# A frequency-domain layer and a selective-scan layer on one core: the second layer's constants and first front issued in turns with the first layer's last synthesis, and a new order for the steady part

## The chip, the core and the metric

The kernel runs on one core of a Trainium2 chip. A core has five engines, each with its own queue of instructions in a fixed order: TensorE (PE: matrix products and transposes into PSUM), VectorE (DVE), ScalarE (ACT), GpSimd (POOL) and SyncE (SP, which here issues most DMAs). Engines wait for each other through semaphores. The metric is the device time of one execution in microseconds (us); lower is better.

## The reference

The input x is 4 images of 192 channels of 128 x 128 points, fp32. Two layers are computed, each as a residual:

```python
x = x + _L0_conv_ref(_gn(x), ...)   # layer 1 in the text: spectra
x = x + _L1_conv_ref(_gn(x), ...)   # layer 2 in the text: selective scan
```

`_gn` is a group norm over groups of 6 channels and all points of an image. The first layer makes 48 channels of the 192, sends 16 through a fractional Fourier transform and back, 16 through a real FFT and back, 16 past both, and projects to 192. The second layer takes each image as a sequence of 16384 tokens. Each token is layer-normed, projected to 384 channels u and 384 gates z; u passes a causal convolution of four taps and a silu. From u come a step size dt (softplus) for each channel and vectors B and C of 16 states for each token. The recurrence, for each of 384 x 16 states along the sequence, is

```python
dA = jnp.exp(dt_t[..., None] * A)
hnew = hcar * dA + (dt_t * u_t)[..., None] * B_t[:, None, :]
y_t = jnp.sum(hnew * C_t[:, None, :], axis=-1)
```

and then y + u * D, times silu(z), projected back to 192 channels, plus the residual.

## The kernel before, in words

**The first layer** (`layer0`) makes four passes per image: `analysis` (statistics and the projection to 48 channels), `forward` and `backward` (the transforms), and `synthesis`, which goes through an image in 16 pieces of 1024 points. For each piece synthesis loads x (`xt`, 768 KB) and the 48 channels (`cat`, four DMAs on SP, two buffers), makes four matrix products (L487), adds them to `xt` on VectorE (L491), takes bn_stats of the sum for the next norm (L202) and stores it to the DRAM tensor `xmid` (L495). `weave` mixes the passes of different images; the last one, synthesis of image 3, runs alone. After it come `bn_done` and `_group_stats`: a chain of small operations on VectorE, PE and ScalarE that gives the norm's mean and scale, `st2`.

**The second layer** (`layer1`) starts then: constants are loaded and prepared, and 128 chunks of 512 tokens follow, 32 to an image. A chunk has 384 channels in three tiles j of 128, 16 states for each: 48 scans of a 128 x 512 tile. They are done in 24 groups of two states; group k is tile j = k // 8 and states 2(k % 8) and 2(k % 8) + 1. The text calls k the place in the chunk. For one state the kernel does:

- the decay exp(dt A) on ScalarE (L875), into SBUF (`da`, AHEAD = 4 states ahead) or into PSUM (`op`);
- the input dt u B, in one of three ways that `KINDS` gives for each group: "V", VectorE multiplies a PSUM copy of dt u with the broadcast B (L896, "product"); "O", GpSimd multiplies both states at once into `db` (L907), with the decay in PSUM; "P", ScalarE scales a transposed dt u (L924, "scale", token by token) and PE transposes it back (L939, `turned_back`);
- the scan on VectorE (L953), into `h`, which has three buffers. The last column of each h is stored by a small DMA on SP as the next chunk's start (`carry`, L964);
- the product with C for both states on GpSimd (`hc`, L966), then the sum over states as transposes that accumulate in PSUM on PE (`sums`, L979, three groups late).

V and P inputs and O decays use three PSUM buffers named `op` in turn. B and C reach the core as a DRAM tensor `dbc`, stored from `xd` on ScalarE's output (`xd_out`) and read back, broadcast over 128 partitions, as up to two loads of 512 KB a group on SP (`load_bc`), at places 19 to 23 and 0 to 2. A new h must wait until both the GpSimd product and the carry store of the h three groups before are done.

**The front** of a chunk (loading `xm`, the norm as a matrix product `to_tokens`, `moments`, `rstd`, `shift`, `normed`, `to_channels`, `channels`, `conv`, `silu_u`, `proj_z`, `silu_z`, `proj_x`, `xd_out`, `proj_dt`, `softplus`, `dt_u`) and its **end** (`evacuate`, `turn`, `gate`, `project_out`, `add_x`) are spread by hand over the groups of the chunks before and after. `PLAN` says where: an entry (at, phase, name, arguments) is issued when the group is `at` places from the chunk's first, so that -35 is place 13 two chunks before. A group has four phases:

```python
act(pos, "S")
turned_back(G * (pos + 1))
... sums ...
act(pos, "A")
... inputs(*order[pos + 2]) ...
scans(pos, n, k, lambda: act(pos, "M"))   # M lies after the first of the two scans
act(pos, "L")
... load_bc ...
```

The order on each engine is this program order (`manual_schedule`), so what an entry puts on an engine stands ahead of all that is issued later. Five PSUM banks serve the plan's other tiles; `psum` takes the bank that was freed first. ScalarE switches its function table between log/exp, silu and softplus (L668, L778, L785, L815).

Of the kernel before, what the change touches and what calls it, by code (L numbers as in the profile page):

```python
# [52 lines left out]
def _group_stats(nc, small, psum, g_ones, mv, out, eps):  # L53

    ps = psum.tile([CH, 512], F32, name="ps")
# [6 lines left out]
    ps2 = psum.tile([CH, 512], F32, name="ps")  # L62
# [59 lines left out]
def layer0(tc, x, xmid, st2, w):  # L122
# [5 lines left out]
    with ExitStack() as ctx:  # L128
        def pool(name, bufs, **kw):
            return ctx.enter_context(tc.tile_pool(name=name, bufs=bufs, **kw))  # L130

        cp = pool("l0c", 1)
        dram = pool("l0d", B, space=DRAM)
        xp = pool("l0x", 7)
        sp = pool("l0s", 2)
# [6 lines left out]
        psB = pool("l0r", 2, space=PSUM)  # L142

        def const(name):
            src = w[name]
            t = cp.tile(list(src.shape), F32, name="c_" + name)
            nc.sync.dma_start(out=t, in_=src)
            return t

        g_ones, w1T, bd, bdb, rm = (const(k) for k in ("g_ones", "w1T", "bd", "bdb", "rowmask"))  # L150
# [5 lines left out]
        w2x = cp.tile([128, C], F32, name="w2x")  # L156
# [24 lines left out]
        cats = [cp.tile([128, 512], F32, name=f"cat{i}") for i in range(2)]  # L181
# [24 lines left out]
        def bn_done(st, out):  # L206
            mv = sp.tile([CH, 2, 2], F32, name="mv")
            for t in range(2):
                nc.vector.bn_aggr(mv[:, t, :], st[:, t, :, :])
            _group_stats(nc, sp, psA, g_ones, mv, out, 1e-5)  # L210
# [46 lines left out]
        def analysis(b, got):  # L257
# [11 lines left out]
            bn_done(st, gst)  # L269
# [3 lines left out]
            w1r = sp.tile([CH, 2, 128], F32, name="w1r")  # L273
# [7 lines left out]
            b1 = sp.tile([128, 1], F32, name="b1")  # L281
            nc.vector.tensor_scalar(b1, ps[:, 0:1], -1.0, None, ALU.mult)
            d1 = got["d1"] = dram.tile([3 * NC, S * S], F32, name="d1")
            for p in (*range(NPIECE - KEEP, NPIECE), *range(NPIECE - KEEP)):
                xt = kept.pop(p, None) or load(b, p)
                if p % 2 == 0:
                    x1 = sp.tile([128, 2, 512], F32, name="x1")
# [184 lines left out]
        def synthesis(b, got, early):  # L472

            d1, dimg = got["d1"], got["dimg"].rearrange("c h w -> c (h w)")
            st = sp.tile([CH, 2, NPIECE * (PIECE // 512), 6], F32, name="st2")
            for p in range(NPIECE):
                xt = early[p] if p < len(early) else load(b, p)
                cat = cats[p % 2]
                for q in range(2):
                    at = slice(p * PIECE + q * 512, p * PIECE + (q + 1) * 512)  # L480
                    nc.sync.dma_start(out=cat[64 * q : 64 * q + NC, :], in_=d1[0:NC, at])
                    nc.sync.dma_start(out=cat[64 * q + NC : 64 * q + 3 * NC, :], in_=dimg[:, at])
# [16 lines left out]
            bn_done(st, st2[:, b])  # L499
# [30 lines left out]
        weave([(synthesis(B - 1, got[B - 1], early), 1)])  # L530
# [4 lines left out]
KINDS = ("VOPPVVOP", "VOVPOVPP", "VOVPPVOP")  # L535

PLAN = (
    (-35, "M", "load_x"), (-34, "M", "to_tokens", 1), (-34, "L", "to_tokens", 0),
    (-33, "L", "moments", 0), (-32, "A", "moments", 1), (-31, "L", "rstd"), (-30, "M", "shift"),
    (-30, "M", "normed", 0), (-30, "M", "normed", 1), (-30, "M", "to_channels", 1),  # L540
    (-29, "L", "to_channels", 0), (-29, "L", "channels", 0), (-27, "L", "channels", 1),
    (-26, "S", "conv", 0, 0), (-26, "L", "conv", 1, 0), (-25, "L", "conv", 1, 1),
    (-24, "L", "conv", 1, 2), (-22, "S", "conv", 0, 1), (-20, "S", "silu_u", 1),
    (-20, "S", "conv", 0, 2), (-20, "S", "silu_u", 0), (-20, "M", "conv", 2, 0),
    (-19, "M", "conv", 2, 1), (-17, "A", "conv", 2, 2), (-16, "L", "silu_u", 2),
    (-15, "L", "proj_z", 0), (-15, "L", "silu_z", 0), (-13, "S", "proj_x"), (-13, "M", "xd_out"),
    (-11, "M", "proj_dt"), (-10, "S", "softplus"), (-9, "M", "dt_u", 1), (-8, "S", "turn_b"),
    (-8, "M", "dt_u", 0), (-8, "M", "b_out"), (-4, "A", "turned", 0), (-2, "M", "scale", 0, 6),
    (-2, "L", "dtu_copy", 0), (-1, "A", "scale", 0, 4), (0, "A", "scale", 0, 5),
    (0, "M", "scale", 0, 15), (1, "S", "scale", 0, 7), (2, "M", "scale", 0, 14),  # L550
    (4, "S", "turned", 1), (7, "A", "dt_u", 2), (7, "A", "dtu_copy", 1), (7, "A", "scale", 1, 6),
    (7, "M", "scale", 1, 7), (9, "M", "scale", 1, 15), (10, "S", "proj_z", 1),
    (10, "A", "scale", 1, 14), (10, "L", "scale", 1, 13), (10, "L", "scale", 1, 12),
    (10, "L", "evacuate", 0), (11, "S", "proj_z", 2), (11, "M", "silu_z", 1),
    (11, "M", "silu_z", 2), (11, "L", "turn", 0), (13, "S", "gate", 0), (13, "A", "dtu_copy", 2),
    (17, "S", "turned", 2), (17, "S", "scale", 2, 6), (17, "M", "scale", 2, 7),
    (18, "M", "scale", 2, 8), (18, "M", "scale", 2, 9), (18, "M", "evacuate", 1),
    (19, "L", "scale", 2, 15), (20, "S", "scale", 2, 14), (21, "A", "turn", 1),
    (22, "S", "gate", 1), (27, "A", "evacuate", 2), (29, "S", "turn", 2), (29, "M", "gate", 2),
    (32, "S", "project_out", 0), (32, "L", "add_x", 0), (34, "S", "project_out", 1),  # L560
# [4 lines left out]
def layer1(tc, xmid, out, st2, w, n_tok=S * S):  # L565
# [6 lines left out]
    AHEAD = 4  # L572
    NBLK = T // 128

    with ExitStack() as ctx:
        def pool(name, bufs, **kw):
            return ctx.enter_context(tc.tile_pool(name=name, bufs=bufs, **kw))

        cp = pool("l1c", 1)
        dram = pool("l1d", 3, space=DRAM)  # L580
# [4 lines left out]
        scp = pool("l1s", 4)  # L585
        op = pool("l1o", 1)
        ps1 = pool("l1p", 1, space=PSUM)
        psa = pool("l1a", 3, space=PSUM)
# [7 lines left out]
        banks = list(range(5))  # L596

        def psum(g, *key):
            bank = banks.pop(0)
            g[key] = ps1.tile([128, 512], F32, name=f"ps{bank}"), bank  # L600

        def done(g, *key):
            banks.append(g.pop(key)[1])
# [8 lines left out]
        nc.vector.scalar_tensor_tensor(  # L612
            nmr, st2[:, :, :, 0], -1.0, st2[:, :, :, 1], ALU.mult, ALU.mult
        )
        dnmr = dram.tile([CH, B, 2], F32, name="dnmr", bufs=1)
        nc.sync.dma_start(out=dnmr, in_=nmr)
        gd = cp.tile([CH + 1, B, 2, CH], F32, name="gd")
        for b in range(B):
# [4 lines left out]
        for b in range(B):  # L623
# [3 lines left out]
        xms = [cp.tile([CH + 1, 2, T], F32, name=f"xm{i}") for i in range(3)]  # L627
        for xm in xms:
            nc.vector.memset(xm[CH : CH + 1], 1.0)
# [40 lines left out]

        def load_x(i):
            b, ch = divmod(i, NCHUNK)
            xm = got[i]["xm"] = xms[i % 3]
            nc.sync.dma_start(
                out=xm[0:CH],
                in_=xmid[b][:, ch * T : (ch + 1) * T].rearrange("(t p) f -> p t f", p=CH),
            )
# [3 lines left out]
        def to_tokens(i, half):  # L681
            g = got[i]
            psum(g, "X", half)
            for blk in (2 * half, 2 * half + 1):
                for t in range(2):
                    nc.tensor.matmul(
                        row(g, blk)[:, t * CH : (t + 1) * CH],
                        g["xm"][:, t, blk * 128 : (blk + 1) * 128], gd[:, i // NCHUNK, t, :],
# [6 lines left out]
        def mean_var(g):  # L695
            return g["X", 1][0][:, 2 * C : 2 * C + 2 * NBLK].rearrange("p (k m) -> p k m", m=2)

        def moments(i, half):
            g = got[i]
            st = tp.tile([128, 2, 6], F32, name="st")  # L700
            for blk in range(2):
                nc.vector.bn_stats(st[:, blk, :], row(g, 2 * half + blk))
            for blk in range(2):
                nc.vector.bn_aggr(mean_var(g)[:, 2 * half + blk, :], st[:, blk, :])

        def rstd(i):
            g = got[i]
# [527 lines left out]
```

## Time and profile before

| | us |
|---|---|
| median of 3 runs (11174.6 to 11181.5) | 11175.6 |
| the profiled execution | 11188.6 |
| its span, first to last instruction | 11186.7 |
| first scan of the second layer | 1445.6 |
| one chunk, mean of 110 | 75.98 |

The page of a profile gives the busy time of each engine, the span in 40 slices, the chain of work that ended last, the costliest groups of instructions and the DMA issues. A line such as `h<-da,carry,op` names what is written and what is read. "Idle before" tells how long an engine stood still before an instruction, with the name of what ended the wait; when an instruction waits for several semaphores, the name is that of the one that came last by the profile, which need not be the one that it needed. PE is TensorE, PEld its weight loads, SPq and POOLq are DMA issues of SyncE and GpSimd.

### The profile page before, as it was taken

Reading aid. Unit: us, or ns where it says so; the run is one execution under the profiler, and the core shown is the slowest. Engines: PE = TensorE matmul, PEld = TensorE weight load, DVE = VectorE, ACT = ScalarE, POOL = GpSimd, SP = SyncE. Lnnn points to the kernel's source line nnn. Section 1 sums busy time; section 2 is a strip of 40 time slices with the busy share of each in tenths; the row PEclk is TensorE's granted clock in tenths of the full one; section 3 lists DMA queues with packets and bytes.
Section 4 is the critical chain, followed back from the end, with each engine's and each line's share of the span. In section 5 each row is a group of like instructions: output and inputs, shape, how many; then the busy total and the mean of one; then the engine's idle time right before and its main releaser. Section 6 shows DMA issues by size and latency. Waiting matters only on the chain. (4 is left out here: it accounts for less than half of the span.)

```text
span 11186.7 us, 171424 instructions
## 1 busy us (share of the span) xinstructions
PE 9950.4 (89%) x56050; PEld 6911.8 (62%) x56050; DVE 10160.0 (91%) x11330; ACT 9542.3 (85%) x20197; POOL 9513.5 (85%) x4342
## 2 busy tenths in 40 slices
PE   4777789999999999999999999999999999999998
PEld 2434356666666666666666666666666666666666
DVE  5666679999999999999999999999999999999999
ACT  2333189999999999999999999999999999999998
POOL 0000079999999999999999999999999999999999
PEclk8888699999999999999999999999999999999999
DMA  8786733333333333333333333333343333333333
GB/s 234 187 225 163 220 98 114 117 105 109 117 105 110 117 105 109 117 112 102 118 117 97 119 119 95 118 119 99 114 119 101 113 117 106 109 117 107 107 117 92
DMA packets 1330364, 1366.48 MB, mean 122 GB/s; under 512 B 918346, under 2 KB 969791, under 8 KB 1328831
## 3 DMA queue, kind: packets, MB, share of 16 engines
q1 hardware_dynamic: 1308990, 1292.60, 39.8%
q0 software_dynamic: 13312, 50.34, 1.4%
q10 hardware_dynamic: 7168, 12.59, 0.3%
q8 instruction: 445, 7.29, 0.3%
q14 instruction: 449, 3.67, 0.1%
HBM read 1179.79 MB, written 155.33 MB: 119 GB/s over the span
## 5 line engine op out<-in xcount | busy, mean ns | idle before, releaser
L966 POOL TENSOR_TENSOR hc<-h,c 128x1024 f32<-128x1024 f32 x3072 | 7200.0, 2367 | 321.2 <-DVE h L953 240.8
L953 DVE TENSOR_TENSOR_SCAN h<-da,carry,op 128x512 f32<-128x512 f32 x4464 | 5532.7, 1268 | 281.0 <-ACT op L875 122.6
L875 ACT ACTIVATE da<-dt,c_A_log 128x512 f32<-128x512 f32 x4608 | 3218.5, 741 | 224.7 <-DVE h L953 216.0
L979 PE MATMUL ps<-ident,hc 128*128 128x128 f32 x24576 | 3258.2, 278 | 3.7 <-POOL hc L966 3.7
L979 PEld LDWEIGHTS ps<-ident,hc 128*128 128x128 f32 x24576 | 2874.5, 144 | 277.2 <-issue 272.2
L924 ACT ACTIVATE dbT<-ps,bT 128x128 f32<-128x128 f32 x9216 | 2583.6, 396 | 12.6 <-PE op L939 11.7
L766 PE MATMUL ps<-s,wc 128*128 128x512 f32 x4608 | 2184.4, 596 | 44.0 <-ACT u L778 36.4
L953 DVE TENSOR_TENSOR_SCAN h<-op,carry,db 128x512 f32<-128x512 f32 x1488 | 1853.4, 1267 | 98.0 <-DMA carry<-h 81.7
L907 POOL TENSOR_TENSOR db<-dtu,b 128x1024 f32<-128x1024 f32 x768 | 1822.5, 2373 | 7.4 <-DMA b<-dbc 7.4
L939 PE MATMUL op<-ident,dbT 128*128 128x128 f32 x9216 | 1422.6, 281 | 242.8 <-ACT dbT L924 168.8
L939 PEld LDWEIGHTS op<-ident,dbT 128*128 128x128 f32 x9216 | 1107.4, 144 | 752.1 <-issue 334.6
L896 DVE TENSOR_TENSOR op<-ps,b 128x512 f32<-128x512 f32 x2304 | 1556.5, 676 | 7.2 <-ACT ps L856 7.2
L875 ACT ACTIVATE op<-dt,c_A_log 128x512 f32<-128x512 f32 x1536 | 1092.0, 711 | 267.4 <-DVE h L953 267.2
L766 PEld LDWEIGHTS ps<-s,wc 128*128 128x128 f32 x4608 | 786.1, 190 | 634.2 <-issue 565.9
L1018 PE MATMUL ps<-yg,c_woT 128*96 128x512 f32 x1536 | 710.2, 599 | 7.6 <-ACT u L778 2.1
L668 ACT ACT_TABLE_LOAD x511 | 655.6, 1283 | 10.0 <-PEq L1225 0.7
L916 PE MATMUL ps<-ident,dtu 128*128 128x128 f32 x1536 | 262.4, 297 | 337.0 <-ACT bT L834 337.0
L822 POOL TENSOR_TENSOR dtu<-dt,u 128x512 f32<-128x512 f32 x384 | 490.6, 1278 | 57.9 <-ACT dt L815 57.9
L495 POOL DMA_DIRECT2D xmid<-xt x64 | 41.6, 651 | 573.2 <-DVE xt L491 528.8
L1018 PEld LDWEIGHTS ps<-yg,c_woT 128*96 128x96 f32 x1536 | 240.2, 163 | 447.7 <-issue 336.7
L916 PEld LDWEIGHTS ps<-ident,dtu 128*128 128x128 f32 x1536 | 179.2, 148 | 393.2 <-ACT bT L834 366.8
L202 DVE BATCH_NORM_STATS2 st<-xt 96x6 f32<-96x512 f32 x512 | 322.2, 677 | 101.7 <-DMA xt<-in_x 100.5
(166 smaller groups left out, 9818.2 us busy)
## 6 DMA issues: line engine op xcount, KB each, us to landing
c<-dbc SPq DMA_DIRECT2D x1024, 512.0 KB, 5.8
b<-dbc SPq DMA_DIRECT2D x768, 512.0 KB, 4.9
xt<-in_x SPq DMA_DIRECT2D x176, 768.0 KB, 8.4
xmid<-xt POOLq DMA_DIRECT2D x64, 768.0 KB, 5.5
xm<-xmid SPq DMA_DIRECT2D x128, 384.0 KB, 3.8
carry<-h SPq DMA_DIRECT2D x3072, 1.0 KB, 1.9
out<-xm SPq DMA_DIRECT2D x128, 384.0 KB, 3.2
s<-s SPq DMA_DIRECT2D x128, 128.5 KB, 2.3
```

What stands on the lines that cost most here:

```text
L668: nc.scalar.preload_act_table_set("natural_log_exp_and_others")
L766: nc.tensor.matmul(g["c", j][0], wc[:, j, k, :], rhs, start=k == 0, stop=k == 5)
L822: nc.gpsimd.tensor_tensor(g["dtu", j], g["dt", j], g["u", j], ALU.mult)
L875: nc.scalar.activation(da, got[n]["dt", j], AF.Exp, scale=A[:, j, st : st + 1])
L896: nc.vector.tensor_tensor(dbs[s], g["dp", j][0], g["b", k % NG][:, q, :], ALU.mult)
L907: nc.gpsimd.tensor_tensor(db, _bc(g["dtu", j], 1, G), g["b", sg], ALU.mult)
L924: nc.scalar.activation(t[:, blk, :], g["tu", j][0][:, at], AF.Identity, scale=g["bT"][:, blk, st : st + 1],)
L939: nc.tensor.transpose(db[:, blk * 128 : (blk + 1) * 128], t[:, blk, :], ident)
L953: nc.vector.tensor_tensor_scan(h[:, q, :], das.pop(s), dbs.pop(s) if db is None else db[:, q, :], 0.0 if ch == 0 else g["before"][:, j, st ...
L966: nc.gpsimd.tensor_tensor(hc, h, g["c", "b", sg], ALU.mult)
L979: nc.tensor.matmul(py[:, blk, :], hc[:, q, blk * 128 : (blk + 1) * 128], ident, start=first, stop=sg == NG - 1 and q == G - 1 and blk == N ...
L1018: nc.tensor.matmul(g["po", t][0][0:CH], woT[:, j, t * CH : (t + 1) * CH], g["yg", j], start=j == 0, stop=j == NJ - 1,)
```

## The change

- `layer0` and `layer1` become generators. The pools of the first layer are split: those that the last synthesis needs stay open, the others are closed before it. The second layer's pools lie on the other side of the memory; its scan pools, one of its PSUM banks and the three `op` buffers are opened only after the last synthesis.
- `program` starts both, so that the second layer's constants are issued before the last synthesis, and then gives the second layer two places of its front after each of the 16 pieces. The front runs so far as place -3 (`LAST`); the group norm of image 3 follows. In the last synthesis the loads of a piece are issued one piece ahead. `_group_stats` takes its PSUM tiles from a function, which gives the last ones from another pool.
- In the steady part: `KINDS` changes for groups 12 (O to V), 20 (P to V) and 21 (V to P). `PLAN` is new throughout. `dbc_out` is an entry of its own, two places after `xd_out`. The residual is loaded a second time, late, into `xr` (28, "M"), and `xm` has one buffer instead of three. Decays in SBUF run seven ahead instead of four. `softplus` is split by tile. `moments` writes to SBUF instead of PSUM, and `rstd` computes its result twice, into SBUF and into PSUM.

In the instruction order of the changed kernel, SP issues 14 loads of B and C of chunk 0 ahead of the four `cat` loads of the last piece.

```diff
-KINDS = ("VOPPVVOP", "VOVPOVPP", "VOVPPVOP")
+BUFS = 7, 3
+
+KINDS = ("VOPPVVOP", "VOVPVVPP", "VOVPVPOP")
 PLAN = (
...
-    (-15, "L", "proj_z", 0), (-15, "L", "silu_z", 0), (-13, "S", "proj_x"), (-13, "M", "xd_out"),
-    (-11, "M", "proj_dt"), (-10, "S", "softplus"), (-9, "M", "dt_u", 1), (-8, "S", "turn_b"),
...
-    (7, "M", "scale", 1, 7), (9, "M", "scale", 1, 15), (10, "S", "proj_z", 1),
-    (10, "A", "scale", 1, 14), (10, "L", "scale", 1, 13), (10, "L", "scale", 1, 12),
-    (10, "L", "evacuate", 0), (11, "S", "proj_z", 2), (11, "M", "silu_z", 1),
...
+    (-15, "A", "proj_z", 0), (-15, "M", "silu_z", 0), (-13, "M", "proj_x"), (-12, "S", "xd_out"),
+    (-11, "M", "proj_dt"), (-10, "S", "dbc_out"), (-10, "A", "softplus", 0),
...
+    (9, "M", "scale", 1, 14), (10, "M", "scale", 1, 13), (10, "L", "scale", 1, 15),
+    (10, "L", "evacuate", 0), (10, "L", "proj_z", 1), (11, "M", "proj_z", 2),
...
+    (26, "M", "evacuate", 2), (28, "M", "load_xr"), (28, "L", "turn", 2), (30, "L", "gate", 2),
+    (31, "S", "project_out", 0), (32, "L", "add_x", 0), (34, "S", "project_out", 1),
...
-    AHEAD = 4
+    AHEAD, H = BUFS
...
-                decay(own[i], scp.tile([128, T], F32, name="da"))
+                decay(own[i], scp.tile([128, T], F32, name="da", bufs=AHEAD))
...
+        def load_xr(i):
+            xr = got[i]["xr"] = op.tile([CH, 2, T], F32, name="xr")
+            nc.sync.dma_start(out=xr, in_=chunk_of(xmid, i))
...
+        def dbc_out(i):
+            g = got[i]
             dbc = g["dbc"] = dram.tile([2, NS, T], F32, name="dbc")
-            nc.sync.dma_start(out=dbc.rearrange("a s t -> (a s) t"), in_=xd[96:, :])
+            nc.sync.dma_start(out=dbc.rearrange("a s t -> (a s) t"), in_=g["xd"][96:, :])
...
-            nc.scalar.activation(rs, mean_var(g)[:, :, 1], AF.Ln, bias=eps)
-            nc.scalar.activation(rs, rs, AF.Exp, scale=-0.5)
+            nc.scalar.activation(lnv, g["mv"][:, :, 1], AF.Ln, bias=eps)
+            g["rp"] = g["X", 1][0][:, 2 * C : 2 * C + NBLK]
+            nc.scalar.activation(rs, lnv, AF.Exp, scale=-0.5)
+            nc.scalar.activation(g["rp"], lnv, AF.Exp, scale=-0.5)
...
         def synthesis(b, got, early):
...
+            def fetch(p):
+                if p < NPIECE:
+                    cat = cats[p % 2]
+                    for q in range(2):
+                        at = slice(p * PIECE + q * 512, p * PIECE + (q + 1) * 512)
+                        nc.sync.dma_start(out=cat[64 * q : 64 * q + NC, :], in_=d1[0:NC, at])
+                        nc.sync.dma_start(out=cat[64 * q + NC : 64 * q + 3 * NC, :], in_=dimg[:, at])
+                if len(early) <= p + len(early) < NPIECE:
+                    xts.append(load(b, p + len(early)))
+
+            if early:
+                fetch(0)
             for p in range(NPIECE):
...
+                fetch(p + 1 if early else p)
...
-        weave([(synthesis(B - 1, got[B - 1], early), 1)])
+        inner.close()
+        yield
+        yield from synthesis(B - 1, got[B - 1], early)
...
             for pos in range(first, 0):
                 for phase in "SAML":
                     act(pos, phase)
                 if pos == -8:
                     for sg in range(NG):
                         load_bc(0, sg)
+                if pos <= LAST:
+                    yield pos == LAST
+                if pos == LAST:
+                    scp = pool("l1s", 4)
+                    op = pool("l1o", 1)
+                    ps2 = pool("l1q", 1, space=PSUM)
+                    psa = pool("l1a", 3, space=PSUM)
+                    banks.append(4)
+                    group_norm(B - 1)
...
-        layer0(tc, x, xmid, st2, w)
-        layer1(tc, xmid, [out[b].rearrange("c h w -> c (h w)") for b in range(B)], st2, w)
+        first = layer0(tc, x, xmid, st2, w)
+        second = layer1(tc, xmid, [out[b].rearrange("c h w -> c (h w)") for b in range(B)], st2, w)
+        next(first)
+        next(second)
+        ready = False
+        for _ in first:
+            for _ in range(2):
+                ready = ready or next(second)
+        for _ in second:
+            pass
```

## The prediction

> **What bounds the kernel now.** I read the page first, then busy time by stretch, VectorE's waits, and the timeline of one chunk and of the passage between the layers.
>
> ```profile
> span 11186.7 us, 171424 instructions
> PE 9950.4 (89%) x56050; PEld 6911.8 (62%) x56050; DVE 10160.0 (91%) x11330; ACT 9542.3 (85%) x20197; POOL 9513.5 (85%) x4342
> ...
> c<-dbc SPq DMA_DIRECT2D x1024, 512.0 KB, 5.8
> b<-dbc SPq DMA_DIRECT2D x768, 512.0 KB, 4.9
> ```
> The shares mix two layers. By stretch (columns: PE, weight loads, VectorE, ScalarE, GpSimd, clock, DMA share, GB/s):
> ```profile
> 1290.00:1310.00 20.00, 14.66 (x33) 4.62 (x29) 18.41 (x25) 0.00 (x0) 2.52 (x4) 0.50 0.95 279
> 1350.00:1370.00 20.00, 13.82 (x24) 4.35 (x20) 18.35 (x27) 0.00 (x0) 2.13 (x4) 0.50 0.69 211
> 1390.00:1410.00 20.00, 12.13 (x34) 7.53 (x35) 2.27 (x10) 8.00 (x13) 0.00 (x0) 0.55 0.03 7
> 1410.00:1430.00 20.00, 17.01 (x43) 6.95 (x42) 0.00 (x0) 6.37 (x9) 0.84 (x1) 0.96 0.10 25
> 1430.00:1450.00 20.00, 13.40 (x44) 8.55 (x44) 7.30 (x15) 12.80 (x33) 5.99 (x4) 0.70 1.00 354
> 5000.00:8000.00 3000.00, 2776.28 (x16289) 1977.01 (x16289) 2871.35 (x3164) 2834.53 (x6096) 2907.32 (x1306) 0.98 0.37 112
> ```
> The last synthesis (to 1370) keeps VectorE at 92% and the DMAs at 95%. Then VectorE and GpSimd stand nearly idle until the first scan at 1445.6. In the steady part (6144 scans, 48 to a chunk; 110 chunks give 75.98 us each) GpSimd is at 97%, VectorE 96%, ScalarE 94%, PE 93%: four engines in lockstep, so single waits matter. VectorE's, over 2000 to 11000 us:
> ```profile
> DVE h L953 <- ACT op L875: 119.3, 120, 1.4
> DVE h L953 <- DMA carry<-h: 101.4, 138, 1.9
> DVE h L953 <- PE op L939: 75.6, 139, 1.1
> DVE h L953 <- POOL hc L966: 33.1, 85, 1.4
> ```
> Summing the timeline's idle before each scan by its place in the chunk (group 0 to 23, mean of 110 chunks) gives 3.16 us a chunk: place 1 0.80, place 3 0.11, place 11 1.00, place 14 0.35, place 15 0.36, place 20 0.45, the rest 0.09. The name at place 11 misleads. One instance:
> ```profile
> 6044.06 2.81 PE L1018 MATMUL ps<-yg,c_woT 128*96 128x512 f32 x6
> ...
> 6046.72 1.02 PE L772 MATMUL ps<-s,wz 128*128 128x512 f32 x2
> 6047.58 1.02 PE L773 MATMUL ps<-s,wz 128*128 128x512 f32 x2
> ...
> 6048.44 0.60 PE L939 MATMUL op<-ident,dbT 128*128 128x128 f32 x4
> 6048.50 0.67 ACT L875 ACTIVATE op<-dt,c_A_log 128x512 f32<-128x512 f32 x1
> ...
> 6049.24 1.28 DVE L953 TENSOR_TENSOR_SCAN h<-da,carry,op 128x512 f32<-128x512 f32 x1 [0.99 <-ACT op L875]
> ```
> That ScalarE write belongs to group 12. Group 11 is a "P" group: its scan needs PE's transposes of 6048.44, which stood behind project_out and proj_z of place 10, phase S. They end at 6049.04; a scan starts some 0.2 us after its PE releaser.
>
> **What the Trainium skill says.** "DMA: Bandwidth & Descriptors", section "Queues, rings and completion order": each DMA engine takes a ring's descriptors in order. The trace agrees: a carry store lands 1.9 us after its issue at places 7 to 10, but 5.16 us at place 22, behind 512 KB B and C loads. "ScalarE: Activation LUTs", section "What ACT_TABLE_LOAD costs": 1283 ns a load (the trace: 1283) plus a drain of 1380 that no row here shows; the next activation starts some 10 ns later. "TensorE: Matmul & The Clock Gate", section "What's actually happening": PE runs at half clock until it is kept busy. The rows agree: 0.50 in the synthesis, 0.98 in the steady part.
>
> **Part 1, the kinds.** Group 12 goes from O to V; groups 20 and 21 swap P and V. GpSimd loses one db product a chunk (2.37 us, start to start 2.33): 0.968 x 75.98 - 2.33 = 71.2 us. VectorE gains two products: in the timeline one moves the next scan's start by 0.58 us, so +1.17. VectorE's work is 75.98 - 3.16 = 72.82, now 73.99: VectorE becomes the bound. ScalarE makes two decays in SBUF (741 ns) instead of PSUM (711) and one more 128x4 exponential (0.2 us); the instruction order holds the same eight table loads a chunk; it stays near 72 us. PE's count is the same, 70.3 us.
>
> **Part 2, the waits.** Place 11: proj_z moves behind the transposes (places 10 L and 11 M), 1.73 us less in front against a stall of 1.00: gone. Place 14 has two parts: 0.17 is the carry of place 11, whose issue waits 4.54 us on the SP queue behind the dbc store, which waits for xd (2.13 to land; 6.67 against the 6.5 us of places 12 and 13). dbc_out now comes two places after xd_out and has nothing to wait for. 0.14 is a late decay; seven ahead instead of four adds three states, over 3.5 us, more than a table switch. Left 0.03. Place 20: group 20 needs no transposes any more and GpSimd is lighter; left 0.10. Place 15 (two P groups in a row, PE late) stays: 0.36. Place 1 is the carry of place 22: issue 1.49 after its scans, behind the s store and two B and C loads, 5.16 to land, 6.65 against 5.9 us of places 23 and 0. That order on SP stays; ScalarE reaches the s store a little earlier: 0.60. GpSimd's sum for places 20 to 1 (two db products in six places) makes it about 0.4 late there, in the same wait, not on top. Places 3 and the rest: 0.21. Sum 1.30, chunk 73.99 + 1.30 = **75.29**, gain 0.69 x 128 = **88 us**. Bounds: no idle left gives 73.99 (-255); all 3.16 left gives 77.15 (+150).
>
> **Part 3, small edits, at nothing.** The second read of the residual is 128 loads of 384 KB where the DMAs are 37% busy, issued at place 4 and used at place 8; uncovered it would cost its landing, 3.8 us a chunk. One xm buffer instead of three: loaded at 13 M, read at 14 L, at least 3.5 us of scans and more on PE; what is uncovered would delay the transposes queued behind. bn_aggr writing SBUF (187 ns to PSUM before) may be 0.05 us either way, four times a chunk, beside idle; up to 26 us over the kernel each way.
>
> **Part 4, the front.** Before: the last bn_stats ends at 1367.0, the statistics at 1371.3, the first scan is at 1445.6 and the first chunk takes 83.5 us where later ones without start-up waits and carries would take 73.0 (48 scans 0.06 shorter): 78.6 + 10.5 = 89 us after the synthesis. After, on the path:
> - the constants (17 SP issues, 2.4 MB at 280 GB/s, 8.6 us) stand before the last image's first pieces, half of them in DMA time that is idle now: +4;
> - VectorE, the bound of the pieces, gets 4.4 us of moments and 2.9 us of weight products: +7;
> - 14 B and C loads (7.3 MB at the 354 GB/s of 1430:1450, 21 us) are issued on SP ahead of the last piece's four loads, while two pieces of 5.2 us are left to compute: +11. This is the queue that the move is dear on;
> - the last image's norm sends two small DMAs on SP ahead of the first carry stores; both are ready with the statistics, and the new pools' first tiles wait for the last stores of the first layer (5.5 us from issue to landing, the last issued near 1365, so before 1371): 0;
> - statistics 4.3, then two table loads (2.6), copies, a scaling, a decay and a product (3.7), start-up waits 3: +14.
>
> Together 36 against 89: 53 gained. PE may be late while both streams share it at a low clock, so I take **45**, with 15 and 70 as ends.
>
> **Sum.** 88 + 45 = 133. The profiled execution took 11188.6 (span 11186.7); the median, 11175.6, is 13 lower and I take the difference off the median: **11043 us**.
>
> **Rivals.**
> *The likeliest*, 0.57: chunk 74.9 to 75.7 with a front gain of 25 to 65: 10973 to 11115.
> *VectorE almost never waits*, 0.13: the seven decays and the lighter GpSimd close nearly all gaps, chunk 74.4: 1.58 x 128 + 45 = 247, 10929. For it: GpSimd drops from 97 to 95%. Against it: four engines above 93% with three-deep h and PSUM buffers.
> *The front alone*, 0.18: waits move to other places, 3.16 - 1.17 = 1.99 us stay, chunk 75.98, only 45 gained: 11131, up to 11155.
> *The front buys nothing*, 0.04: the synthesis waits for front work in PE's and SP's order as long as it saves; 88 left: 11088, within the first case's times.
> *Slower: PE late at places 13 to 15*, 0.08. Groups 12 and 13 are now V and 14 and 15 P; proj_z 1 and 2, proj_x and project_out lie at places 10 and 11. By the rates in the timeline (0.43 us for a 512-wide matmul, 0.11 for a transpose) PE has 13.8 us at places 10 to 12 against 10.6 of VectorE's: 3.1 late at place 13, and with 0.46 for the transposes 1.2 past place 13's 2.4. Again at 14: 0.6. That would be 1.5 more than the 0.36 taken, chunk 76.75, +99 - 45 = +54: 11230. It decides from 1.2 more idle a chunk (156 us) on. Against it: the same sum for the kernel before (3.9 late, 3.0 of scans) gives 1.4 where 0.35 was seen, so it overstates by 1 us.
>
> **How the numbers follow.** A measurement of this kernel can tell about 0.2% (22 us) from no change. Range **10935 to 11150**: the likeliest case and the emptied front whole (0.61), half of the second (0.06), most of the third (0.15). Faster by over 0.2%: 0.57 + 0.13 + 0.04 + 0.14 = 0.88; within: 0.04; slower: 0.08.
>
> **What would show it.** Steady chunk near 75.3 us, GpSimd under 96%, VectorE near 98%; no idle at place 11, little at 14 and 20, some left at 1 and 15; carry stores of places 11 and 12 issued at once; the first scan at 1395 to 1415, after a gap before the last piece of about 10 us filled by B and C loads. Wrong if VectorE's idle stays near 2 us or above, or if the last synthesis grows by over 40 us.

## The result and the profile after

The changed kernel takes 11222.45 us (median of 5 runs, 11219.08 to 11247.99), the kernel before 11175.64 beside it: a ratio of 1.0043, 95% interval 1.0028 to 1.0058. It is slower; 11043 and the range to 11150 were wrong. The profiled executions say the same: spans of 11217.3 and 11186.7 us.

The page of the changed kernel has new line numbers: the scan is L984 (was L953), the decay L906 (L875), the product L927 (L896), `turned` L947 (L916), `turned_back` L970 (L939), `hc` L997 (L966), `sums` L1010 (L979), `turn` L1035 (L1004), `gate` L1042 (L1011).

```profile
span 11217.3 us, 171938 instructions
PE 10022.3 (89%) x56050; PEld 7046.3 (63%) x56050; DVE 10265.6 (92%) x11587; ACT 9573.1 (85%) x20327; POOL 9223.7 (82%) x4214
...
c<-dbc SPq DMA_DIRECT2D x1024, 512.0 KB, 6.0
b<-dbc SPq DMA_DIRECT2D x768, 512.0 KB, 5.0
...
xr<-xmid SPq DMA_DIRECT2D x128, 384.0 KB, 4.9
```

GpSimd has lost 290 us of work, as the kinds say. TensorE has the same 56050 matrix products as before and yet 72 us more of busy time: on average each takes longer. Busy time by stretch (columns as before the change):

```profile
1290.00:1310.00 20.00, 17.20 (x50) 6.22 (x49) 17.34 (x23) 2.72 (x3) 2.63 (x5) 0.93 0.88 271
1350.00:1370.00 20.00, 3.88 (x10) 0.80 (x6) 6.49 (x16) 2.37 (x8) 2.04 (x3) 0.50 1.02 399
1370.00:1390.00 20.00, 11.12 (x26) 6.08 (x27) 11.37 (x19) 4.13 (x8) 2.99 (x2) 0.51 0.24 71
1390.00:1410.00 20.00, 15.25 (x51) 8.24 (x50) 14.38 (x15) 19.02 (x43) 11.59 (x5) 0.83 0.04 2
5000.00:8000.00 3000.00, 2781.59 (x16121) 2003.05 (x16119) 2876.20 (x3207) 2814.81 (x6066) 2789.28 (x1254) 0.96 0.39 116
```

Two things are to be seen. The stretch that stood empty before is filled, and scans run in 1390 to 1410. And in the steady part TensorE's granted clock is 0.96 where it was 0.98: at half clock for the rest, that is 0.04 x 2 x 76.65 = 6 us a chunk instead of 3.

The front, in VectorE's timeline:

```profile
1375.81 1.22 DVE L510 TENSOR_TENSOR xt<-xt,pr 96x1024 f32<-96x1024 f32 x1 [19.31 <-PE pr L506]
...
1385.53 0.16 DVE L638 SCALAR_TENSOR_TENSOR nmr<-st 96x2 f32<-96x2 f32 x1
...
1393.63 2.33 DVE L984 TENSOR_TENSOR_SCAN h<-da,op 128x512 f32<-128x512 f32 x2 [4.29 <-ACT da L906]
```

The first scan is at 1393.6, 52.0 us earlier; the first chunk takes 78.3 us instead of 83.5. From the start of the last scan 20.8 us follow instead of 16.6. So the ends gain 53 us, and the steady part loses more: the mean chunk is 76.65 us, before 75.98; 128 x 0.67 is 86. Together +33, by the spans +30.6.

VectorE's waits over 2000 to 11000 us:

```profile
DVE yg L1042 <- PE ps L1035: 105.1, 116, 1.3
DVE h L984 <- PE op L970: 75.7, 188, 0.5
DVE h L984 <- DMA carry<-h: 68.0, 89, 2.4
DVE h L984 <- issue: 45.7, 52, 1.5
DVE h L984 <- ACT dbT L955: 31.4, 24, 1.7
DVE h L984 <- ACT da L906: 14.0, 26, 0.9
DVE h L984 <- POOL hc L997: 10.4, 11, 2.1
```

The first line is new. It is `gate 1` in place 21, which waits for TensorE's transposes of `turn 1`; before, the wait of a `gate` was 5.9 us in all. VectorE's idle time by place, us a chunk, is the same reading as in the prediction (e1 and e9 are experiments below):

| place | before | predicted | after | e1 | e9 |
|---|---|---|---|---|---|
| 1 | 0.80 | 0.60 | 0.83 | 1.38 | 1.36 |
| 3 | 0.11 | 0.11 | 0.20 | 0.07 | 0.09 |
| 11 | 1.00 | 0 | 0 | 0 | 0 |
| 14 | 0.35 | 0.03 | 0.01 | 0.01 | 0.01 |
| 15 | 0.36 | 0.36 | 0.47 | 0.47 | 0.47 |
| 20 | 0.45 | 0.10 | 0 | 0 | 0 |
| 21 | 0 | 0 | 1.23 | 0 | 0.15 |
| 23 | 0 | 0 | 0.23 | 0.23 | 0.25 |
| sum, rest included | 3.16 | 1.30 | 3.09 | 2.24 | 2.44 |
| chunk less idle | 72.82 | 73.99 | 73.57 | 73.31 | 73.37 |

Now TensorE's timeline, of one chunk before, from place 14 on:

```profile
6672.57 0.60 PE L829 MATMUL ps<-ident,xd 128*128 128x128 f32 x4
6673.00 1.04 PE L979 MATMUL ps<-ident,hc 128*128 128x128 f32 x8
6676.71 0.66 PE L916 MATMUL ps<-ident,dtu 128*128 128x128 f32 x4 [2.67 <-ACT bT L834]
6677.20 1.14 PE L979 MATMUL ps<-ident,hc 128*128 128x128 f32 x8
6680.05 1.09 PE L939 MATMUL op<-ident,dbT 128*128 128x128 f32 x4 [1.71 <-ACT dbT L924]
```

and of the same part of a chunk after:

```profile
6657.09 0.66 PE L860 MATMUL ps<-ident,xd 128*128 128x128 f32 x4
...
6661.28 0.60 PE L947 MATMUL ps<-ident,dtu 128*128 128x128 f32 x4
6661.71 1.04 PE L1010 MATMUL ps<-ident,hc 128*128 128x128 f32 x8
6666.71 1.09 PE L970 MATMUL op<-ident,dbT 128*128 128x128 f32 x4 [3.96 <-DVE h L984]
6667.59 1.92 PE L1010 MATMUL ps<-ident,hc 128*128 128x128 f32 x8
```

The same eight `sums` transposes take 1.04 us before the idle stretch and 1.92 after it, the four of `turned_back` 1.09 instead of 0.60: TensorE has dropped to half clock. Its idle time a chunk is unchanged (stretches over 0.2 us: 5.40 before, 5.43 after), but the two longest stretches, 2.67 and 1.62 (medians), have become 3.96 and 0.74. `turned 2` (L947) no longer waits for the B transposes to be copied out of their bank (`bT`), because `turn_b` and `b_out` come earlier, and it is itself issued two phases earlier (16 M instead of 17 S); so TensorE runs dry until a scan of place 17 frees an `op` buffer. By the trace's clock records half clock takes 3.29 us a chunk before, in 65% of the chunks, and 5.74 after, in 96%, from place 17 or 18 on. Chunks with it take 76.70 us after, those without 75.35, but the latter are four chunks only; e5 below has 55 of each. In the kernel before the same two kinds of chunk take 76.13 and 75.71, so the new order also pays more for a dip than the old one did. Place 21 comes while TensorE is still behind:

```profile
6677.40 0.69 DVE L1042 TENSOR_TENSOR yg<-ps,zs 128x512 f32<-128x512 f32 x1 [0.77 <-PE ps L1035]
```

### The profile page after: what moved, and what is told of

Read it like the earlier page. It is cut to its first block, busy times and chain, and to the rows that moved or that the text cites. A ratio compares the mean times of both kernels' runs of the same rounds, so it can differ in the third digit from the quotient of the medians.

```text
span 11217.3 us, 171938 instructions
## 1 busy us (share of the span) xinstructions
PE 10022.3 (89%) x56050; PEld 7046.3 (63%) x56050; DVE 10265.6 (92%) x11587; ACT 9573.1 (85%) x20327; POOL 9223.7 (82%) x4214
## 5 line engine op out<-in xcount | busy, mean ns | idle before, releaser
L997 POOL TENSOR_TENSOR hc<-h,c 128x1024 f32<-128x1024 f32 x3072 | 7218.1, 2367 | 691.6 <-DVE h L984 572.5
L984 DVE TENSOR_TENSOR_SCAN h<-da,carry,op 128x512 f32<-128x512 f32 x4712 | 5846.4, 1267 | 157.3 <-PE op L970 78.9
L906 ACT ACTIVATE da<-dt,c_A_log 128x512 f32<-128x512 f32 x4864 | 3394.9, 737 | 75.4 <-DVE h L984 68.0
L1010 PE MATMUL ps<-ident,hc 128*128 128x128 f32 x24576 | 3270.7, 281 | 5.7 <-POOL hc L997 4.8
L1010 PEld LDWEIGHTS ps<-ident,hc 128*128 128x128 f32 x24576 | 2919.1, 146 | 279.4 <-issue 257.4
L795 PE MATMUL ps<-s,wc 128*128 128x512 f32 x4608 | 2141.1, 596 | 57.1 <-ACT s L780 57.1
L970 PE MATMUL op<-ident,dbT 128*128 128x128 f32 x9216 | 1500.7, 288 | 612.3 <-DVE h L984 588.2
L970 PEld LDWEIGHTS op<-ident,dbT 128*128 128x128 f32 x9216 | 1137.6, 148 | 1004.8 <-ACT dbT L955 556.0
L927 DVE TENSOR_TENSOR op<-ps,b 128x512 f32<-128x512 f32 x2560 | 1727.2, 675 | 6.4 <-ACT ps L887 1.0
L984 DVE TENSOR_TENSOR_SCAN h<-op,carry,db 128x512 f32<-128x512 f32 x1240 | 1542.3, 1269 | 109.1 <-DMA carry<-h 51.3
L938 POOL TENSOR_TENSOR db<-dtu,b 128x1024 f32<-128x1024 f32 x640 | 1515.0, 2367 | 6.1 <-DVE nmr L638 6.1
L795 PEld LDWEIGHTS ps<-s,wc 128*128 128x128 f32 x4608 | 806.6, 191 | 761.2 <-issue 684.8
L906 ACT ACTIVATE op<-dt,c_A_log 128x512 f32<-128x512 f32 x1280 | 906.7, 708 | 219.8 <-DVE h L984 219.3
L1019 ACT COPY yt<-ps 128x512 f32<-128x512 f32 x384 | 226.4, 590 | 283.0 <-PE ps L1010 282.2
L1025 PE MATMUL ps<-ddp,u 128*128 128x128 f32 x3072 | 446.1, 293 | 0.0
```

Source lines behind the costliest of these rows:

```text
L795: nc.tensor.matmul(g["c", j][0], wc[:, j, k, :], rhs, start=k == 0, stop=k == 5)
L906: nc.scalar.activation(da, got[n]["dt", j], AF.Exp, scale=A[:, j, st : st + 1])
L927: nc.vector.tensor_tensor(dbs[s], g["dp", j][0], g["b", k % NG][:, q, :], ALU.mult)
L938: nc.gpsimd.tensor_tensor(db, _bc(g["dtu", j], 1, G), g["b", sg], ALU.mult)
L970: nc.tensor.transpose(db[:, blk * 128 : (blk + 1) * 128], t[:, blk, :], ident)
L984: nc.vector.tensor_tensor_scan(h[:, q, :], das.pop(s), dbs.pop(s) if db is None else db[:, q, :], 0.0 if ch == 0 else g["before"][:, j, st ...
```

## The experiments

**The theory**: the moved entries `turn_b`, `b_out` and `turned 2` merge TensorE's idle time, its clock halves, and it is late for the gate of place 21. **Rivals**: the gate itself stands too early in place 21; or the new kinds and the deeper decays are what costs, whatever the clock.

All runs in one table. "Before" on those chips was 11186.12 (e1 to e4), 11184.07 (e5 to e8) and 11186.01 (e9 to e12), so the ratios are what compares. Chunk and idle are VectorE's, us, mean of 110 chunks; stretch is TensorE's longest idle stretch of a chunk (median); half is the share of chunks with half clock. The filler is e1's edit: transposes that are repeated for no other purpose than to keep TensorE busy.

| run | kernel | us | ratio, 95% interval | chunk | idle | stretch | half |
|---|---|---|---|---|---|---|---|
| before | - | 11175.64 | 1 | 75.98 | 3.16 | 2.67 | 65% |
| after | the change | 11222.45 | 1.0043 (1.0028 to 1.0058) | 76.65 | 3.09 | 3.96 | 96% |
| e1 | after, with the filler | 11080.48 | 0.9905 (0.9891 to 0.9918) | 75.55 | 2.24 | 1.36 | 1% |
| e2 | after, gate 1 later | 11236.58 | 1.0050 (1.0038 to 1.0063) | 76.87 | 3.36 | 3.98 | 98% |
| e3 | e1 and e2 | 11105.14 | 0.9926 (0.9913 to 0.9940) | 75.65 | 2.32 | 1.34 | 0% |
| e4 | after, with old kinds, plan, decays | 11102.05 | 0.9926 (0.9913 to 0.9938) | 75.70 | 3.34 | 2.19 | 46% |
| e5 | after, shorter filler | 11136.77 | 0.9958 (0.9942 to 0.9975) | 75.93 | 2.48 | 2.67 | 50% |
| e6 | e1, `s` store on ScalarE | 11202.56 | 1.0016 (1.0008 to 1.0025) | 76.64 | 3.02 | 1.89 | 39% |
| e7 | e6 and e12 | 11117.53 | 0.9943 (0.9928 to 0.9958) | 75.82 | 2.09 | 0.96 | 23% |
| e8 | e1, moments in PSUM | 11125.49 | 0.9949 (0.9934 to 0.9964) | 75.89 | 2.26 | 1.68 | 5% |
| e9 | after, three entries put back | 11117.78 | 0.9943 (0.9930 to 0.9955) | 75.81 | 2.44 | 2.15 | 29% |
| e10 | e1, group 12 on GpSimd | 11094.93 | 0.9922 (0.9910 to 0.9935) | 75.78 | 3.53 | 1.47 | 5% |
| e11 | e1, decays four ahead | 11081.09 | 0.9906 (0.9891 to 0.9921) | 75.57 | 2.29 | 1.37 | 2% |
| e12 | e1, TensorE's order changed | 11102.85 | 0.9931 (0.9919 to 0.9943) | 75.69 | 2.31 | 0.75 | 15% |

**e1: work in the stretch.** The four transposes of `turned 2` are repeated, so that TensorE has something to do there; they write the same values again.

```diff
-            for blk in range(NBLK):
+            for blk in [*range(NBLK)] * (7 if j == 2 else 1):
```

> The changed kernel with the four transposes of dt u of tile 2 (place 16, phase M) repeated seven times: 24 more transposes of 0.11 us, 2.6 us a chunk, into the same PSUM tile, in time in which TensorE now stands idle for 3.9 us before the transposes of group 19. The output is the same. Theory 'clock' (that idle stretch lets TensorE's clock fall to half in 96% of the chunks, so it is late at places 18 to 21, the turn of tile 1 comes late and VectorE's gate waits for it): half clock in few chunks, idle at place 21 from 1.23 to below 0.3 us, chunk from 76.65 to about 75.4, time 11222 - 150 = about 11070. Theory 'gate' (the gate of tile 1 was put half a place too near its turn, whatever the clock): 2.6 us more work on TensorE, no gain, 11210 to 11260.

11080.48 is 142 us below the kernel after (1.4%, or 154 us, by the two ratios), and it was won by adding work to a busy engine. TensorE's timeline of e1 at the same place as above:

```profile
6584.32 3.22 PE L947 MATMUL ps<-ident,dtu 128*128 128x128 f32 x28
6587.38 1.04 PE L1010 MATMUL ps<-ident,hc 128*128 128x128 f32 x8
6589.77 0.63 PE L970 MATMUL op<-ident,dbT 128*128 128x128 f32 x4 [1.36 <-DVE h L984]
6590.24 1.04 PE L1010 MATMUL ps<-ident,hc 128*128 128x128 f32 x8
```

The sums after the stretch keep their 1.04 us. Busy time of e1 by stretch:

```profile
5000.00:8000.00 3000.00, 2850.45 (x17307) 2051.31 (x17306) 2910.52 (x3256) 2851.30 (x6163) 2833.11 (x1274) 1.00 0.39 117
```

The clock is 1.00, the wait at place 21 is gone (table above). The theory holds.

**e2: the gate later**, and **e3: both.**

```diff
-    (21, "A", "turn", 1), (21, "M", "gate", 1),
+    (21, "A", "turn", 1), (22, "S", "gate", 1),
```

> The changed kernel with one entry of the plan moved: the gate of tile 1 from place 21 phase M back to place 22 phase S, as in the kernel before, a scan later. Theory 'gate': the 0.87 us that VectorE waits for the turn goes and nothing takes its place, chunk 75.8, time 11222 - 110 = about 11110. Theory 'clock': the half clock stays in nearly all chunks; the wait of the gate goes, but TensorE is still late, the 0.36 us at the first scan of place 21 stays and part of the 0.87 comes back at places 22 and 23, chunk 76.0 to 76.4, time 11140 to 11190.

> Both edits at once: the repeated transposes and the gate at place 22 phase S. If the clock causes the wait, moving the gate adds nothing to the filler alone: within 15 us of it, about 11070. If both count for themselves: 11222 - 150 - 50 = about 11020. What is left then is idle at places 1, 3 and 15, 1.5 us a chunk.

e2's wait at the gate is gone and nothing is gained. VectorE's waits in e2, 2000 to 11000 us:

```profile
DVE h L984 <- PE op L970: 186.3, 235, 1.3
DVE h L984 <- issue: 99.0, 120, 1.8
...
DVE yg L1042 <- PE ps L1035: 1.9, 3, 0.7
```

The idle went to places 22 (0.47) and 23 (1.12), which wait for TensorE too: the gate was only the first to meet a late engine. With the filler the later gate gains nothing either. This rival falls.

**e4: the front and the small edits, with the old kinds, plan and decays.**

```diff
-BUFS = 7, 3
-KINDS = ("VOPPVVOP", "VOVPVVPP", "VOVPVPOP")
+BUFS = 4, 3
+KINDS = ("VOPPVVOP", "VOVPOVPP", "VOVPPVOP")
...
+    (-13, "M", "xd_out"), (-13, "M", "dbc_out"),
...
+    (28, "M", "load_xr"), (29, "S", "turn", 2),
```

> The changed kernel with the steady part of the kernel before: its kinds, its plan, decays four ahead; dbc_out stands again right behind xd_out, softplus for the three tiles in one place, the second read of the residual at place 4 (28, M) and the one xm buffer stay. Theory 'the front is worth what its trace shows': first scan at about 1394 instead of 1446, chunk 75.98 as before, time 11176 - 50 = about 11125. Rival 'the small edits cost' (one xm buffer, the second read, the moments in SBUF): chunk above 76.2, 11150 and more.

0.9926: without the new steady part the change gains. The first scan is at 1402.6, and the chunk falls to 75.70 with the old order: VectorE's work falls from 72.82 to 72.36, and its idle grows by 0.18. From start to next start (idle left out), the four bn_aggr of a chunk take 0.44 us instead of 0.77 and the four bn_stats 1.05 instead of 1.20, which is about all of that fall: it is the move of the moments to SBUF (e8). The new steady part costs 1.0043 - 0.9926 = 1.2%, 131 us.

**e5: a shorter filler**, `* (4 if j == 2 else 1)` instead of 7.

> The changed kernel with the transposes of tile 2 repeated four times instead of seven (12 more, 1.3 us; seven times gave 11080 with no half clock in the steady part). The idle stretch of TensorE shrinks from 3.9 to 2.6 us, the length that the longest one of the kernel before has, where 65% of the chunks show half clock. Theory 'a stretch of idle time of a certain length, not the sum of work, sets the clock': half clock in 40 to 80% of the chunks, chunk 75.8 to 76.3, 11110 to 11170. Rival 'any filling is enough': none, 11080.

The stretch is 2.67 us, half of the chunks have half clock, and the time lies between: a dose and its response. In e5 chunks with half clock take 76.61 us, those without 75.26 (55 of each).

**e9: the three entries put back**, no filler.

```diff
-    (-10, "L", "turn_b"), (-10, "L", "b_out"),
+    (-8, "S", "turn_b"), (-8, "M", "b_out"),
...
-    (16, "M", "turned", 2),
+    (17, "S", "turned", 2),
```

> The kernel after, without extra transposes, with three entries of the plan put back to their places of before: turn_b at (-8, S), b_out at (-8, M), turned 2 at (17, S). Clock theory: the moves of these entries (and not the new kinds) merged TensorE's idle of places 16 to 19 into one stretch of 3.9 us; put back, the idle is split again, half-clock time falls from 5.7 to 2 to 4 us a chunk, in 50 to 75% of chunks; the idle at place 21 falls from 1.23 to 0.5 or less, the chunk from 76.65 to 75.9 to 76.2, time 11120 to 11170. Rival, the kinds make the stretch (group 20 needs no transposes any more, so that TensorE has nothing to do there): the stretch stays over 3.4 us, half clock in over 90% of chunks, time 11200 to 11240.

TensorE's timeline of e9 at the same place:

```profile
6606.48 1.04 PE L1010 MATMUL ps<-ident,hc 128*128 128x128 f32 x8
6609.67 0.66 PE L947 MATMUL ps<-ident,dtu 128*128 128x128 f32 x4 [2.16 <-ACT bT L865]
6610.17 1.15 PE L1010 MATMUL ps<-ident,hc 128*128 128x128 f32 x8
6612.93 1.09 PE L970 MATMUL op<-ident,dbT 128*128 128x128 f32 x4 [1.62 <-DVE h L984]
```

The stretch is in two again, with as much idle time in all (5.60). Half clock falls to 29% of the chunks, below what I expected, and the time to 0.9943: these three entries, which change no amount of work, cost 1.0%, 112 of the 131 us. That the new kinds make the stretch falls.

**The clock records, window by window.** In each of the 14 traces all changes of the clock lie on one grid of 3.413 us (within 1.1 ns). TensorE's busy share can be counted in each window of that grid, over the same 110 chunks of every trace. Of 33473 windows at full clock, 424 had a share under 0.40, and half clock followed every one of them. It followed 24 of the 40 windows from 0.40 to 0.42, and 79 of the 33009 above. Two windows of the kernel before, each with the one behind it (columns as above):

```profile
5080.56:5083.97 3.41, 1.53 (x12) 1.29 (x12) 3.41 (x5) 3.18 (x9) 3.41 (x3) 1.00 0.04 0
5083.97:5087.39 3.42, 2.10 (x16) 1.72 (x16) 3.42 (x5) 3.39 (x15) 3.42 (x2) 1.00 0.04 0
5230.74:5234.16 3.42, 1.22 (x11) 1.22 (x12) 3.42 (x4) 3.00 (x7) 3.42 (x3) 1.00 0.00 0
5234.16:5237.57 3.41, 1.77 (x9) 1.41 (x8) 3.41 (x5) 3.38 (x15) 3.41 (x3) 0.50 0.08 1
```

The first has TensorE busy for 1.53 us (0.45), and full clock follows; the third for 1.22 us (0.36), and half clock follows. So what counts is how much of one window is idle: more than 0.60 of it, 2.05 us. An estimate from these figures: a stretch of s us (2.05 or more), with TensorE busy around it, leaves such a window in (s - 0.69) / 3.41 of its positions on the grid. That is 0.96 for 3.96 us, 0.58 for 2.67, 0.43 for 2.15 and none for 1.36; measured are 96%, 65 and 50%, 29% (46% for e4's 2.19) and 1%. This is why the same idle time costs more in one piece. e6's median of 1.89 us hides a mixture: each of its 35 windows under 0.40 holds one idle piece of over 2.05 us.

**e6: the `s` store on ScalarE's queue**, with the filler, against the carry of place 22 that ends place 1's wait.

```diff
-                nc.sync.dma_start(out=s[64:128, 1, 1 : T + 3], in_=s[0:64, 1, 0 : T + 2])
+                nc.scalar.dma_start(out=s[64:128, 1, 1 : T + 3], in_=s[0:64, 1, 0 : T + 2])
```

> The filler (seven times) and the store of s (128 KB) issued by ScalarE, which makes s, instead of SyncE. Theory 'place 1 waits for the carry store of place 22, which stands on SyncE's queue behind the store of s (issued 2.2 us after the scans of place 22, 5.3 us to land, against 6.0 us of scans)': the carry is issued at once, idle at place 1 from 1.38 to 0.3 us, chunk 74.5, 11080 - 135 = about 10945. Rival 'it is ScalarE's decays for the O group that are late, as the name in the profile (ACT dbT) says, or GpSimd's': idle at place 1 stays above 1 us, ScalarE loses 0.1 to 0.5 us a chunk to the issue, 11080 to 11120.

The carry store now issues 0.04 us after its scans (2.24 in e1), and place 1's idle falls from 1.38 to 0.25: the cause at place 1 is right. But the `s` store itself now lands 5.9 us after its issue, against 2.3 in e1 (medians), and TensorE's `conv` (L795), which never waited for it in e1, waits 145 us for it from 2000 to 11000 us. Place 2 gets 1.42, half clock comes back in 39% of the chunks, now from place 1 on, and the whole is 1.1% slower than e1. The store's new queue closed one wait and opened another, with TensorE's next stretch in it.

**e7: e6 with TensorE's order changed**, and **e12: that order without e6**.

```diff
-    (-26, "A", "conv", 1, 0),
+    (-26, "L", "conv", 1, 0),
...
-    (-11, "M", "proj_dt"), (-10, "S", "dbc_out"), (-10, "A", "softplus", 0),
+    (-10, "S", "dbc_out"), (-10, "A", "proj_dt"), (-10, "M", "softplus", 0),
```

> As the one with the store of s on ScalarE, and two pieces of TensorE work moved behind transposes that a scan waits for: proj_dt from place 13 phase M to place 14 phase A (softplus of tile 0 to phase M), the first part of conv 1 from place 22 phase A to phase L. Theory 'the 0.47 us at place 15 and the 0.22 at place 23 are TensorE's order, as place 11 was in the kernel before': both under 0.1, chunk 0.55 us shorter than without, 70 us: about 10875. Rival 'the PSUM buffers come free too late': no change, 10945.

> The kernel of e1 with proj_dt one place later (with softplus 0 behind it, -10 M) and conv 1,0 one phase later (-26 L), as in e7 but with the s store left on SP. In e7 this took away the idle at place 15 (0.47 us a chunk). If it does so here with no new stretch of TensorE's idle: chunk 75.0 to 75.2, time 11020 to 11050. If idle moves to other places or half clock comes back (e7: 0.39 at place 21, 0.57 at place 2): chunk 75.4 to 75.8, 11070 to 11115. I take the first, 11045, at six in ten.

Place 15's idle of 0.47 is gone in both, so `proj_dt` in front of the transposes was its cause. The time doesn't follow: e12 is at 0.9931, e1 at 0.9905. VectorE's waits in e12, 2000 to 11000 us:

```profile
DVE h L984 <- DMA carry<-h: 119.6, 91, 3.0
DVE h L984 <- ACT dbT L955: 65.3, 40, 3.0
DVE yg L1042 <- PE ps L1035: 44.5, 115, 1.3
```

Place 1 has 1.63, place 21 0.40, and half clock returns from place 19 on in 15% of the chunks, though the longest stretch of a chunk is only 0.75 us in the median: its length isn't all that decides. Of the 16 times that half clock begins in e12, 15 follow a window that begins in place 18 and holds `to_channels`, whose four transposes wait one by one for ScalarE; so do 22 of e7's 25. The profile counts 0.30 us as busy for each of these transposes, where eight in a row take 1.04, so those windows, at 0.6 to 0.7, are less busy than they look. That this brings them under 0.40 isn't shown.

**e8: the moments in PSUM again**, with the filler.

```diff
-                nc.vector.bn_aggr(g["mv"][:, 2 * half + blk, :], st[:, blk, :])
+                nc.vector.bn_aggr(mean_var(g)[:, 2 * half + blk, :], st[:, blk, :])
```

> The filler (seven times), with the moments, rstd and shift of the kernel before: mean and variance written to PSUM instead of SBUF, one exponential less. Theory 'writing them to SBUF is what shortens VectorE's work by 0.45 us a chunk (76.65 - 3.09 = 73.57 after; 72.82 + 1.17 = 73.99 expected)': VectorE's work back to 74.0, chunk 76.0, 11080 + 58 = about 11140. Rival 'no difference': 11080.

The chunk less idle grows from 73.31 to 73.63, the time by 45 us. bn_aggr to PSUM takes 187 ns and waits 27 ns for the one before; to SBUF it takes 173 and waits for nothing. Four a chunk make 0.16 of the 0.32 by these rows. Counted from start to next start, the four bn_aggr of a chunk take 0.64 us against 0.45 in e1 and the four bn_stats in front of them 1.18 against 1.06: together the 0.32.

**e10: group 12 on GpSimd again**, and **e11: decays four ahead**, both with the filler.

```diff
-KINDS = ("VOPPVVOP", "VOVPVVPP", "VOVPVPOP")
+KINDS = ("VOPPVVOP", "VOVPOVPP", "VOVPVPOP")
```

```diff
-BUFS = 7, 3
+BUFS = 4, 3
```

> The kernel of e1 (extra transposes in turned 2) with group 12 back to O, so that GpSimd makes its db product and VectorE two products less. The prediction's price: VectorE's work 1.17 us less a chunk, GpSimd's 2.33 more. If VectorE is the bound and its idle stays at 2.2: chunk 74.4, time 10935. If GpSimd at its old load is as near the bound as it was (before: 97%, idle of VectorE 3.16): idle grows by about as much as the work shrinks, chunk 75.3 to 75.9, time 11050 to 11130. I take the second, 11085.

> The kernel of e1 with decays four ahead instead of seven. The prediction said that three more states ahead save 0.14 us a chunk (a late decay at place 14), 18 us in all: chunk 75.6 to 75.75, time 11085 to 11110, with waits for a decay (ACT da) at a place behind a table switch. Rival: the deep decays hide more, since ScalarE does all eight table loads a chunk in front of scans: over 0.4 us a chunk, time over 11130.

In e10 VectorE's work falls by 1.07 us, its idle grows by 1.29. Its waits, 2000 to 11000 us:

```profile
DVE yg L1042 <- PE ps L1035: 112.1, 119, 1.6
DVE h L984 <- DMA carry<-h: 94.0, 79, 2.8
```

0.95 of that is `gate 0` at the end of place 12: the place is two products shorter, so the gate comes 1.1 us sooner than before, and TensorE's transposes for it don't. So with this plan and at full clock the new kind is worth 0.22 us a chunk; in time that is 0.2%, no more than a measurement can tell. e11 is the same as e1: the deep decays do nothing that a time shows.

The fastest version that was run is e1 (and e11): 0.9905 of the kernel before.

## Why the prediction was wrong

*The front* was right. Worked at 53, taken at 45: the first scan is 52.0 us earlier, with the first chunk 57. One execution says no more than that, though: in the profiles of the twelve experiments, whose front is the same or nearly so, the first scan lies between 1394.8 and 1412.0, and the median of all thirteen is 1399.9, 46 us gained. Inside it the gap before the last piece was 19 us, filled with B and C loads at 399 GB/s as said, not 10; other terms must have been smaller by at least as much. They weren't followed singly, so it is in part luck that the sum came out. The 4 us of a longer end weren't foreseen.

*Part 1* was right. VectorE's two products were priced at 1.17 us; e10 measures 1.07. GpSimd is at 93% of the stretch, under the 96% given.

*Part 2 is the step that failed.* Of the waits that it named, places 11, 14 and 20 went as it said, and the carry stores of 11 and 12 issue 0.03 us after their scans. Places 1, 3, 15 and 23 came out 0.66 higher together. The failure is its sum: 1.30 counts the old waits that stay and gives the new order none, and place 21 took 1.23. It asked of TensorE only how much work stood in front of a scan; it did not ask where TensorE would stand still. `turn_b`, `b_out` and `turned 2` appear in no line of it, since no wait of VectorE's ended with them; e9 gives them 1.0% of the time. With the clock whole (e1) the chunk is 75.55 against 75.29 forecast, and the time 0.9905 against 0.9881.

That e1 comes so near is partly luck: its work is 0.68 lower than forecast, its idle 0.94 higher, 0.78 of it at place 1. And e9, without a filler, has a chunk of 75.81 against e4's 75.70: there the new kinds and order trade 1.0 us more work (73.37 against 72.36) for 0.9 less idle, which is the rival "the front alone", put at 0.18.

*Part 3*: the moments were set at nothing, with 0.05 us either way four times a chunk as bounds. e8 measures 0.32 a chunk, 45 us, outside the 26 given, and the kernel gained it: a term mis-sized, though not the one that failed. Part 2's 0.14 for deeper decays at place 14 isn't seen in e11.

*The rivals.* The slower one, at 0.08, had 11230 and the engine right, and place and cause wrong: TensorE was said to be late by a queue of work at 13 to 15, where the idle fell from 0.71 to 0.48 (only place 15 rose, by 0.11). It was late from having had nothing to do. The view that would have told: the granted clock of 0.98 in the steady part, which the prediction quoted as agreement with the Trainium skill ("TensorE: Matmul & The Clock Gate", section "What's actually happening"). 0.98 is not full: it is 3 us a chunk at half clock. The same section says that half clock follows an idle window of about 3.4 us. The traces agree on the window, 3.413 us, and differ on "idle": a window under 0.40 busy was enough, 424 times of 424, which a stretch of 2.67 us brings about in 50 to 65% of the chunks.

Open: whether the windows of e12 and e7 before half clock are truly under 0.40 busy, why the new order pays more for half clock than the old, and whether place 1's 1.38 can be closed without opening TensorE's next stretch.

## What to carry to other kernels

When entries of a queue are moved, write down where the engine will stand still as well as where it will be late: TensorE's idle time in one piece costs more than the same time in two. A granted clock of 0.98 in a stretch is worth resolving by place, and a few idle transposes are a cheap test: here 24 of them a chunk took 142 us off the changed kernel, 1.3% as timed. A wait that an edit removes is worth its length only if the engine behind it has slack; e2 closed one and gained nothing, e6 and e12 closed one and lost.

## What the hardware showed that was not expected

- TensorE's clock changes on a grid of 3.413 us. Half clock followed each of the 424 windows in which TensorE was busy for less than 0.40 of the time, though it stood idle throughout (under 0.02) in only 57 of them, and 0.2% of those with 0.42 or more. At half clock it stayed after all 112 windows under 0.70 busy, and ended after 525 of the 629 with 0.80 or more; so in the steady part it comes in pieces of 3.41, 6.83 or 10.24 us.
- At half clock eight 128 x 128 transposes take 1.92 us instead of 1.04. The 6.0 us of it in a chunk (5.74 in the mean, in 96% of chunks) put TensorE at most some 3 us behind, by estimate; the chunk pays 1.35 us of that (76.70 against 75.35, and 76.61 against 75.26 in e5).
- Four bn_aggr a chunk, with the bn_stats in front of them, are cheaper to SBUF than to PSUM by 0.32 us, twice what the rows of bn_aggr alone show (0.16).
- The 128.5 KB store of `s` landed 5.9 us after its issue on ScalarE's queue and 2.3 us on SP's (e6 against e1).
